# Sums with the unit matrix kept in the order of the text on VectorE, in a two-layer graph network kernel

## The chip, the cores and the metric

The kernel runs on one core of a Trainium2 chip. The metric is the device time of one execution in microseconds (us), and the median of three runs is given. A profile of one more execution shows what each engine did: TensorE (PE, with its weight loads as PEld), VectorE (DVE), ScalarE (ACT), GpSimd (POOL) and SyncE (SP), which issues most DMAs. All data are float32.

## The reference, cut to what matters

The input is x, 128 graphs of 128 nodes with 256 channels, and adj, an adjacency matrix of 128 x 128 for each graph. There are two layers, each with a layer norm and a residual around it. Layer 0 joins a convolution over the nodes, a message-passing product and a gated recurrent unit, for all nodes. Layer 1 touches the first 25 nodes of each graph. It works on five groups of them (25, 9, 7, 6 and 6 nodes), and each group has two graph convolutions with normalised adjacency:

```python
A = adj + jnp.eye(n, dtype=adj.dtype)
deg = jnp.sum(A, axis=-1)
...
norm_adj = dinv[:, :, None] * A * dinv[:, None, :]
support = jnp.einsum('bnd,de->bne', x, W)
out = jnp.einsum('bnm,bme->bne', norm_adj, support) + b
return jax.nn.relu(out)
```

The sum adj + eye is what the change is about. It is needed twice: once for the first convolution and once for the second.

## The kernel before, in words

The 128 graphs are worked on in 32 blocks of four graphs. A first phase (up to about 440 us) makes the convolution of layer 0 by way of spectra; it is not touched here. Then comes a loop over the 32 blocks. For each block `gates(i, ...)` computes the recurrent unit in four units (`unit`, lines 709 to 743): each is a product by Strassen's scheme, seven sums of matmuls (line 719), each in its own PSUM bank. What comes out of a bank goes to ACT (`m1`, line 722, and `m5`, line 730), DVE (lines 724, 727, 734, 737, 740) and POOL (lines 732, 738). There are eight banks, and a matmul that opens a bank has to wait until the former content was read. The first unit of a block writes tile `o` (or `r`), followed by a sigmoid in two halves on ACT (line 755); the next ones write `nh`, `nn` and `z`.

Between the seven sums of a unit, `step()` lets other work go on, all of it written as Python generators: `beside_gates` (the messages, the edge terms, the convolution's output and, in `back`, the end of the block two before) and, once all blocks of a part are done, `layer1` of that part. The parts have 40, 40, 36 and 12 graphs (`PARTS`), so that layer 1 of a part runs beside the gates of a few later blocks, and the last part at the very end. Blocks beside which no layer 1 runs are called plain blocks here.

`back(i, ae, dc)` prepares layer 1 of a block: it adds the residual (line 860), takes the first 25 nodes out (`xl`, line 870), and then adds the unit matrix `ie` to the block's edges `ae` (line 876, 100 x 212) and scales the five groups of it by `dinv` (line 879). A few steps later it makes the layer norm of these nodes (lines 886 to 892: statistics on DVE, a power on POOL, a product on ACT into `hn`), multiplies `hn` by `ae` on PE (line 896) and scales the result (line 901). `ae` has one buffer; it is loaded on SP (line 851) as soon as the L896 of the block before has read it.

In `layer1` the second convolution goes by packs: 60 diagonal blocks of graphs of one group, at most 128 wide. `prepare(j)` (lines 911 to 928) does three things when pack j's turn comes: it issues the load of adjacency `nt` of pack j+8 (line 918) and of its scale `dck` (line 921) on SP, and on DVE it adds the unit matrix `ident` to pack j+2's `nt` (line 925) and multiplies it by `dck` (line 926). `last` reads `nt` in a matmul (line 967), adds bias and relu on ACT (line 970), and sums into `f` on DVE (line 975). Line 987 is the matmul of the first convolution, line 1046 that of the second's support.

The order of the instructions on each engine is not the text's alone. A planner places them when the program is built: an instruction whose inputs it takes as ready may float ahead of others on its engine. `tc.keep_in_program_order(ins)` pins one behind what the text has issued last on the same engine. On POOL the whole first phase and a few more places are in the order of the text. At run time each engine works through its own queue in order.

The wrappers that the change touches, as they stand before:

```python
nc.vector.tensor_add(ae[:n4], ae[:n4], ie[:n4])
...
ops = [nc.vector.tensor_add(nt[:n, :n], nt[:n, :n], ident[:n, :n]),
       nc.vector.tensor_mul(nt[:n, :n], nt[:n, :n], dc[:n, :n])]
tc.keep_in_program_order(ops[1])
```

Here the product (`ops[1]`) is pinned behind the sum, and the sum is not pinned.

Of the kernel before, what the change touches and what calls it, by code (L numbers as in the profile page):

```python
# [77 lines left out]
def gnn_kernel(ctx: ExitStack, tc: tile.TileContext, io, out0: bass.AP, out1: bass.AP):  # L78
    nc = tc.nc
# [13 lines left out]
    def bank():  # L93
        pool, n = banks
        if n is None:
            return pool.tile([P, 512], F32, tag="bank", name="bank")
        banks[1] = (n + 1) % 8
        return pool.tile([P, 512], F32, tag=f"bank{n}", name="bank")
# [10 lines left out]
    ident = cst.tile([P, P], F32)  # L109
# [670 lines left out]
    n4 = BB * NN  # L780
# [5 lines left out]
    ie = l1.tile([P, GW], F32)  # L786
# [69 lines left out]
    def back(i, ae, dc):  # L856

        xt, o = xts.pop(i), outs.pop(i)
        for c in range(C):
            nc.vector.tensor_add(xt[:, c, :], xt[:, c, :], o[:, c, :])  # L860
        xv = xt.rearrange("p c (b n) -> p c b n", b=BB)
        k, b0 = where[i]
        if k == LAST:
            if not kept:
                kept["f"] = l1.tile([P, C, PARTS[k], NN], F32, tag="fl", name="fl", bufs=1)
                kept["ax"] = l1.tile([P, C, PARTS[k] // BB * GW], F32, tag="axl", name="axl", bufs=1)
            xl = kept["f"][:, :, b0:b0 + BB, :]
        else:
            xl = wk.tile([P, C, BB, NN], F32, tag="xl", name="xl", bufs=2)
        nc.vector.tensor_copy(xl, xv[:, :, :, :NN])  # L870
        yield

        nc.sync.dma_start(out0[i], xv[:, :, :, NN:])
        if k != LAST:
            nc.sync.dma_start(xf[k][:, :, b0:b0 + BB, :], xl)
        nc.vector.tensor_add(ae[:n4], ae[:n4], ie[:n4])
        for g in range(len(GROUPS)):
            av = ae[:n4, GOFF[g]:GOFF[g + 1]]
            nc.vector.tensor_scalar(av, av, dinv[:n4, E0 + 5 * i + g:E0 + 5 * i + g + 1], None, op0=ALU.mult)
        yield  # L880
        ps = bank()
        for c in range(C):
            nc.tensor.transpose(ps[:n4, c * P:(c + 1) * P], xl[:, c].rearrange("p b m -> p (b m)"), ident)
        st = l1.tile([P, 6], F32, tag="st", name="st", bufs=2)
        mv = l1.tile([P, 4], F32, tag="mv1", name="mv1", bufs=2)
        nc.vector.bn_stats(st[:n4], ps[:n4, :D])
        nc.vector.bn_aggr(mv[:n4, 0:2], st[:n4])
        nc.vector.tensor_scalar(mv[:n4, 2:3], mv[:n4, 1:2], EPS, None, op0=ALU.add)
        nc.gpsimd.tensor_tensor(mv[:n4, 3:4], mv[:n4, 2:3], mhalf[:n4, 0:1], op=ALU.pow)
        hn = l1.tile([P, D], F32, tag="hn", name="hn", bufs=1)  # L890
        nc.vector.tensor_scalar(hn[:n4], ps[:n4, :D], mv[:n4, 0:1], 0.0, op0=ALU.subtract, op1=ALU.max)
        nc.scalar.mul(hn[:n4], hn[:n4], mv[:n4, 3:4])
        yield
        ps = bank()
        for c in range(C):
            nc.tensor.matmul(ps[:, c * GW:(c + 1) * GW], hn[:n4, c * P:(c + 1) * P], ae[:n4], start=True, stop=True)  # L896
        if k == LAST:
            ab = kept["ax"][:, :, b0 // BB * GW:(b0 // BB + 1) * GW]
        else:
            ab = l1.tile([P, C, GW], F32, tag="ab", name="ab", bufs=1)  # L900
        nc.vector.tensor_tensor(ab, ps[:, :C * GW].rearrange("p (c m) -> p c m", c=C),
                                dc[:, None, :].to_broadcast([P, C, GW]), op=ALU.mult)
        if k != LAST:
            for g, (s, _) in enumerate(GROUPS):
                at = PARTS[k] * GOFF[g] // BB + b0 * s
                nc.sync.dma_start(xa[k][:, :, at:at + BB * s], ab[:, :, GOFF[g]:GOFF[g + 1]])
        yield
# [3 lines left out]
    def prepare(j):  # L911

        a = j + AHEAD
        if 0 <= a < NPK:
            s, nb = GROUPS[PACKS[a][1][0]][0], PACKS[a][1][2]
            n = nb * s
            nt = l1.tile([P, P], F32, tag="nt", name="nt", bufs=AHEAD + 4)
            ins = nc.sync.dma_start(nt[:n, :n], io["adjN"][a, :n, :n])
            tc.keep_in_program_order(ins)
            dc = l1.tile([P, P], F32, tag="dck", name="dck", bufs=AHEAD)  # L920
            nc.sync.dma_start(dc[:n, :n], dvk[a, :n].partition_broadcast(n))
            loads1[a] = n, nt, dc
        if 0 <= j + 2 < NPK:
            n, nt, dc = loads1.pop(j + 2)
            ops = [nc.vector.tensor_add(nt[:n, :n], nt[:n, :n], ident[:n, :n]),
                   nc.vector.tensor_mul(nt[:n, :n], nt[:n, :n], dc[:n, :n])]
            tc.keep_in_program_order(ops[1])
            ready[j + 2] = nt

    def weights(ws, name, bufs, shape, upto):  # L930
# [13 lines left out]
    def layer1(k):  # L944
# [56 lines left out]
        if k == 0:  # L1001
            weights1(3)
            weights2(3)
            for q in (-2, -1):
                prepare(q)
# [9 lines left out]
        for n, chunk in enumerate(chunks):  # L1015
# [12 lines left out]
            for t in range(len(segs) + 1):  # L1028
                if t < len(segs):
                    g, m0, _ = segs[t]  # L1030
                    m1 = bounds[t + 1]
                    if k == LAST:
                        xv = kept["ax"].rearrange("p c (b m) -> p c b m", m=GW)
                        xv = xv[:, :, :, GOFF[g]:GOFF[g + 1]]
                    else:
                        xv = axs[n][:, :, m0:m1]
                    yield from first(g, m0, m1, xv)
                if t:
                    g, _, packs = segs[t - 1]
                    for b0, nb, at, jj in packs:  # L1040
                        prepare(jj)
                        n1 = nb * GROUPS[g][0]
                        nt = ready.pop(jj)
                        ps = bank()
                        for q in range(HID // P):
                            nc.tensor.matmul(ps[:n1, :D], hh[:, q, at:at + n1], w2s[k5 + g][:, q, :],  # L1046
                                             start=q == 0, stop=q == HID // P - 1)
                        s2 = l1.tile([P, D], F32, tag="s2", name="s2", bufs=3)
                        nc.scalar.mul(s2[:n1, :], ps[:n1, :D], dinv[:n1, K0 + jj:K0 + jj + 1])
                        if late:  # L1050
                            late.pop(0)()
                        late.append(partial(last, g, b0, nb, s2, nt))
                        if jj == ends[g]:
                            weights2(k5 + g + 4)
                        yield
# [10 lines left out]
    def beside_gates(i):  # L1066

        ends = back(i - 2, *back_loads(i - 2)) if i > 1 else iter(())
        if i < NBLK:
            parts = messages(i)  # L1070
            next(parts)
            yield
            next(parts)
            next(ends, None)
            yield
            next(ends, None)
            yield
            edge_terms(i)
            next(ends, None)
            yield  # L1080
            for _ in range(3 if i > 1 else 0):
                yield
            next(ends, None)
            yield
            pss = short_rows(i)
            yield
            for _ in conv_out(i, pss):
                yield
            yield from x_nmp(i)
        for _ in ends:  # L1090
            yield
            if i == NBLK:
                yield
# [42 lines left out]
    for i in range(NBLK):  # L1136
# [28 lines left out]
        if (i + 2) * BB == PARTS[0]:  # L1165
            for q in range(-AHEAD, -2):
                prepare(q)
        for k in range(len(PARTS)):
            if i * BB == first_of[k + 1]:
                layer1s.append(layer1(k))  # L1170

    end = back(NBLK - 1, *back_loads(NBLK - 1))
    next(end)
    for steps in (6, 4):
# [145 lines left out]
```

## Time and profile before

| what | value |
|---|---|
| median of three runs (lowest, highest) | 1830.15 us (1829.33, 1830.82) |
| the profiled execution's own time | 1828.48 us |
| its span, first to last instruction | 1826.6 us |
| granted TensorE clock | 0.999 |
| L876 `ae` sum on DVE | 32 times, 366 to 381 ns |
| L879 `ae` scale on DVE | 160 times, 222 to 798 ns, median 234 |
| L925 `nt` sum on DVE | 60 times, 221 to 772 ns, median 278 |
| L926 `nt` product on DVE | 60 times, 218 to 817 ns, median 280 |

Times inside the profile are counted from the first instruction. A line of the groups or the timeline names the source line, the engine, the operation, the tile written and those read (`o<-bank,u`), the shapes and the count. An idle time in square brackets or after a bar is the engine's idle time just before, with what is held to have ended it; where an instruction waits for several things, the view names one of them. Matmuls are pipelined: float32 matmuls show as two passes, a pass of 128 x 256 lasts 379 ns in the records, and the next one starts before it has ended, so starts tell more than the busy share.

### The profile page before, as it was taken

What the parts mean: (1) busy time and instruction counts of PE and PEld (TensorE: products, weight loads), DVE (VectorE), ACT (ScalarE), POOL (GpSimd) and SP (SyncE); (2) the same over time, 40 slices, a digit from 0 to 9 for tenths busy, and PEclk for the clock granted to TensorE, in tenths of its full rate; (3) what the DMA queues carried; (4) which work ended last, traced back from release to release, by engine and by line L of the source; (5) the groups of instructions that cost most, each with busy time, mean ns of one, the idle gap of its engine ahead of it and who ended that gap; (6) DMA issues with size and microseconds to landing.
All of it is one profiled execution on the core that took longest, in us unless ns stands there. A gap on an engine that the chain in (4) does not pass through costs nothing.

```text
span 1826.6 us, 34568 instructions
## 1 busy us (share of the span) xinstructions
PE 1807.0 (99%) x12552; PEld 1565.5 (86%) x12552; DVE 1359.7 (74%) x3248; ACT 737.4 (40%) x1626; POOL 789.0 (43%) x993
## 2 busy tenths in 40 slices
PE   9999999999999999999999999999999999999998
PEld 7888888888888888888788888888788888888787
DVE  6989956787978878877665687878656677887552
ACT  5766721113433433343344434343343433333334
POOL 4777765774354435443221244344313244444100
PEclk9999999999999999999999999999999999999999
DMA  7989889996533343433243433334434434332034
GB/s 292 354 327 340 336 304 322 344 307 211 144 80 74 79 96 74 92 100 94 64 111 104 121 85 85 72 82 110 88 82 91 132 84 94 74 84 73 22 90 139
DMA packets 279869, 267.46 MB, mean 146 GB/s; under 512 B 170870, under 2 KB 247371, under 8 KB 277651
## 3 DMA queue, kind: packets, MB, share of 16 engines
q1 hardware_dynamic: 272211, 211.67, 41.6%
q10 hardware_dynamic: 7488, 53.58, 7.5%
q8 instruction: 100, 1.64, 0.4%
q14 instruction: 70, 0.57, 0.1%
HBM read 168.84 MB, written 96.35 MB: 145 GB/s over the span
## 4 chain that ended last, share of the span: by engine, by line
PE 90%; DVE 4%; DMA 2%; POOL 1%; SPq 1%; issue 1%; ACT 1%; ACTq 0%; DVEq 0%; POOLq 0%
PE bank L719 43%; PE bank L377 6%; PE bank L256 6%; PE bank L1046 6%; PE bank L987 5%; PE bank L620 5%; PE bank L372 3%; PE bank L670 3%; PE bank L599 3%; PE bank L182 2%; PE bank L285 2%; PE bank L967 1%; PE bank L240 1%; PE bank L896 1%; DMA nt<-in_adjN_dram 1%
## 5 line engine op out<-in xcount | busy, mean ns | idle before, releaser
L732 POOL TENSOR_TENSOR u<-u,m 128x256 f32<-128x256 f32 x128 | 95.1, 743 | 458.6 <-ACT m L730 397.0
L719 PE MATMUL bank<-t,sw 128*128 128x256 f32 x1152 | 291.8, 380 | 0.7 <-DVE nn L734 0.3
L719 PEld LDWEIGHTS bank<-t,sw 128*128 128x128 f32 x1152 | 214.5, 190 | 33.6 <-issue 2.8
L719 PE MATMUL bank<-t,wih 128*128 128x256 f32 x768 | 200.2, 383 | 0.0
L719 PEld LDWEIGHTS bank<-t,wih 128*128 128x128 f32 x768 | 143.1, 190 | 29.3 <-DVE o L759 5.3
L369 POOL TENSOR_TENSOR vs<-v 128x256 f32<-128x256 f32 x134 | 101.6, 783 | 53.8 <-PE bank L372 26.0
L256 PE MATMUL bank<-wc,ht 128*128 128x256 f32 x512 | 124.4, 391 | 0.3 <-issue 0.3
L719 PE MATMUL bank<-xc,wih 128*128 128x256 f32 x384 | 114.8, 380 | 0.1
L719 PE MATMUL bank<-t,whh 128*128 128x256 f32 x384 | 114.5, 380 | 0.0
L719 PE MATMUL bank<-xn,wih 128*128 128x256 f32 x384 | 114.2, 379 | 0.0
L1046 PE MATMUL bank<-w,hh 128*125 128x256 f32 (+9 forms) x480 | 113.4, 380 | 0.1
L719 PE MATMUL bank<-ht,whh 128*128 128x256 f32 x384 | 110.4, 380 | 0.1
L603 ACT ACTIVATE xc<-xc,bn 128x512 f32<-128x512 f32 x64 | 46.2, 722 | 158.6 <-DVE xc L602 158.5
L643 ACT ACTIVATE msg<-msg 128x512 f32<-128x512 f32 x64 | 36.8, 622 | 179.3 <-DVE msg L639 179.3
L256 PEld LDWEIGHTS bank<-wc,ht 128*128 128x128 f32 x512 | 93.9, 191 | 16.2 <-issue 0.7
L1046 PEld LDWEIGHTS bank<-w,hh 128*125 128x125 f32 (+9 forms) x480 | 84.4, 178 | 18.2 <-DVE hh L992 1.2
L987 PE MATMUL bank<-ax,w 128*128 128x500 f32 (+9 forms) x352 | 94.5, 404 | 0.9 <-DVE xc L602 0.9
L772 ACT ACT_TABLE_LOAD x31 | 39.8, 1283 | 117.0 <-DVE z L740 117.0
L737 DVE TENSOR_TENSOR u<-bank,u 128x256 f32<-128x256 f32 x128 | 53.4, 417 | 44.9 <-PE bank L719 44.5
L374 ACT COPY k<-bank 128x256 f32<-128x256 f32 x67 | 24.9, 372 | 145.9 <-PE bank L372 76.2
L719 PEld LDWEIGHTS bank<-xn,wih 128*128 128x128 f32 x384 | 72.9, 190 | 10.0
L719 PEld LDWEIGHTS bank<-xc,wih 128*128 128x128 f32 x384 | 72.1, 190 | 9.8 <-ACT m L722 1.9
(225 smaller groups left out, 4563.9 us busy)
## 6 DMA issues: line engine op xcount, KB each, us to landing
vd<-sp ACTq DMA_DIRECT2D x16, 2176.0 KB
v<-vd SPq DMA_DIRECT2D x34, 1024.0 KB
w<-in_w_dram SPq DMA_DIRECT2D x40, 512.0 KB
ln<-in_x_dram SPq DMA_DIRECT2D x32, 512.0 KB
htd<-ht SPq DMA_DIRECT2D x32, 512.0 KB
yd<-ys ACTq DMA_DIRECT2D x32, 512.0 KB
ht<-htd SPq DMA_DIRECT2D x64, 256.0 KB
ym<-yd SPq DMA_DIRECT2D x32, 512.0 KB
```

What stands on the lines that cost most here:

```text
L256: nc.tensor.matmul(pv[:, s, :], ht[:, c, (2 * h + s) * N:(2 * h + s + 1) * N], wc1[:, c, :], start=c == 0, stop=c == C - 1)
L369: nc.gpsimd.tensor_tensor(vs[:, c], vi[c], vr[c], op=ALU.subtract)
L372: nc.tensor.matmul(p1[:, :D], a[:, c], vs[:, c], start=c == 0, stop=c == C - 1)
L377: nc.tensor.matmul(ps[:, k * D:(k + 1) * D], u[:, c], w[c], start=c == 0, stop=c == C - 1)
L599: nc.tensor.matmul(ps[:, b * N:(b + 1) * N], ym[:, 2 * h + b, o * P:(o + 1) * P], idm, start=False, stop=b == 1)
L620: nc.tensor.matmul(ps[:, b, :], d[:, b * N:(b + 1) * N], w, start=True, stop=True)
L670: nc.tensor.matmul(ps[:, b * N:(b + 1) * N], msg[:, b, c * P:(c + 1) * P], e[:, b, :], start=True, stop=True)
L719: nc.tensor.matmul(ps, w, d, start=n == 0, stop=n == len(pairs) - 1)
L732: nc.gpsimd.tensor_tensor(got["u4"], got["u2"], got["m5"], op=ALU.add)
L737: nc.vector.tensor_tensor(got["u3"], ps, got["u2"], op=ALU.add)
L987: nc.tensor.matmul(pv[:, q - q0, :], w1s[k5 + g][:, c, q * P:(q + 1) * P], xv[:, c], start=c == 0, stop=c == C - 1)
L1046: nc.tensor.matmul(ps[:n1, :D], hh[:, q, at:at + n1], w2s[k5 + g][:, q, :], start=q == 0, stop=q == HID // P - 1)
```

## The change

The sum of `ae` and `ie` and that of `nt` and `ident` are both pinned in the order of the text. The product in `prepare` was pinned already and stays so. Nothing is added to or taken from the work. The text of the change has one line less, so lines after 925 are one lower in it (L967 becomes L966); lines are named by the numbers of the kernel before unless said otherwise.

```diff
@@ -873,7 +873,7 @@
         nc.sync.dma_start(out0[i], xv[:, :, :, NN:])
         if k != LAST:
             nc.sync.dma_start(xf[k][:, :, b0:b0 + BB, :], xl)
-        nc.vector.tensor_add(ae[:n4], ae[:n4], ie[:n4])
+        tc.keep_in_program_order(nc.vector.tensor_add(ae[:n4], ae[:n4], ie[:n4]))
         for g in range(len(GROUPS)):
             av = ae[:n4, GOFF[g]:GOFF[g + 1]]
             nc.vector.tensor_scalar(av, av, dinv[:n4, E0 + 5 * i + g:E0 + 5 * i + g + 1], None, op0=ALU.mult)
@@ -922,9 +922,8 @@
             loads1[a] = n, nt, dc
         if 0 <= j + 2 < NPK:
             n, nt, dc = loads1.pop(j + 2)
-            ops = [nc.vector.tensor_add(nt[:n, :n], nt[:n, :n], ident[:n, :n]),
-                   nc.vector.tensor_mul(nt[:n, :n], nt[:n, :n], dc[:n, :n])]
-            tc.keep_in_program_order(ops[1])
+            tc.keep_in_program_order(nc.vector.tensor_add(nt[:n, :n], nt[:n, :n], ident[:n, :n]))
+            tc.keep_in_program_order(nc.vector.tensor_mul(nt[:n, :n], nt[:n, :n], dc[:n, :n]))
             ready[j + 2] = nt
 
     def weights(ws, name, bufs, shape, upto):
```

## The prediction

> **What bounds the kernel now.** I read the page first. TensorE (PE) is busy for the whole span and VectorE (DVE) for three quarters of it:
>
> ```profile
> PE 1807.0 (99%) x12552; PEld 1565.5 (86%) x12552; DVE 1359.7 (74%) x3248; ACT 737.4 (40%) x1626; POOL 789.0 (43%) x993
> ```
>
> A busy PE may still be a waiting one, so I went on to the busy time by stretches, cut at the first L896 matmul of neighbouring blocks (columns: length, then busy time of PE, PEld, DVE, ACT, POOL). 36.12 us is the length of most blocks in which no layer-1 work runs. Three of those shown are longer:
>
> ```profile
> 705.42:741.53 36.11, 36.11 (x211) 32.20 (x210) 29.41 (x67) 14.01 (x28) 15.71 (x20) 1.00 0.35 80
> 741.53:781.08 39.55, 37.64 (x212) 32.03 (x211) 33.32 (x83) 13.89 (x28) 16.69 (x20) 1.00 0.39 88
> ...
> 1248.14:1285.39 37.25, 36.84 (x212) 32.03 (x211) 30.27 (x71) 13.89 (x28) 16.58 (x20) 1.00 0.45 120
> 1644.04:1682.53 38.49, 37.38 (x212) 32.11 (x210) 30.00 (x71) 13.89 (x28) 16.25 (x20) 1.00 0.29 78
> ```
>
> In the plain blocks PE is tight: the chain of the end runs through PE alone there, and its longer pieces hold 18 passes of L719 in 3.89 us or 24 in 5.18 us, 0.216 us each in both. So a DVE delay that reaches PE is lost time, and there is little to win: about 8 us, in the long blocks, as worked out below. What makes them long is in the waits of DVE (total, times, longest):
>
> ```profile
> DVE nt L925 <- DMA nt<-in_adjN_dram: 50.2, 27, 4.5
> ...
> DVE ae L876 <- DMA ae<-in_adjE_dram: 9.4, 7, 2.9
> ```
>
> **What the change moves.** It adds and removes no instruction. Set against each other, the two built programs have the same order on PE, ACT and POOL. On DVE the six instructions of `ae` (L876 and five L879) and the 60 pairs L925/L926 stand elsewhere; on SP the `dck` loads (L921) come later, because each waits for the L926 that frees its buffer.
>
> *The place of ae.* In the plain blocks before, the six stand between L727 and L587 of the next-gate unit (1107.9 us in the block I follow). In the change they stand 28 us later, in the next block, between L734 and L737 of the first gate unit (tile `o`). So I priced the new place with the rows of that place before. First the length of the set, from DVE's timeline, where POOL is idle beside it and where it is not:
>
> ```profile
> 1034.70 0.37 DVE L876 TENSOR_TENSOR ae<-ae,ie 100x212 f32<-100x212 f32 x1
> 1035.11 0.85 DVE L879 TENSOR_SCALAR ae<-ae,dinv 100x100 f32<-100x100 f32 x5
> 1035.87 0.42 DVE L587 TENSOR_TENSOR e<-e,at 128x256 f32<-128x256 f32 x1
> ```
> ```profile
> 1107.92 0.37 DVE L876 TENSOR_TENSOR ae<-ae,ie 100x212 f32<-100x212 f32 x1
> 1108.32 1.37 DVE L879 TENSOR_SCALAR ae<-ae,dinv 100x100 f32<-100x100 f32 x5
> 1109.61 0.41 DVE L587 TENSOR_TENSOR e<-e,at 128x256 f32<-128x256 f32 x1
> ```
>
> Start to next start: 1.17 us alone; 1.69 us when one L879 stands still (752 ns instead of about 230) until POOL's L732 ends at 1109.52. Now the new place, in the timelines of DVE, POOL, ACT and PE:
>
> ```profile
> 1099.75 0.42 DVE L734 TENSOR_TENSOR o<-bank,u 128x256 f32<-128x256 f32 x1 [1.12 <-PE bank L658]
> 1100.10 0.41 DVE L737 TENSOR_TENSOR u<-bank,u 128x256 f32<-128x256 f32 x1
> ```
> ```profile
> 1098.99 0.73 POOL L732 TENSOR_TENSOR u<-u,m 128x256 f32<-128x256 f32 x1 [3.17 <-ACT m L730]
> 1100.59 0.73 POOL L738 TENSOR_TENSOR o<-u,m 128x256 f32<-128x256 f32 x1 [0.87 <-DVE u L737]
> ```
> ```profile
> 1101.35 0.72 ACT L755 ACTIVATE o<-o,brz 128x512 f32<-128x512 f32 x1 [0.16 <-POOL o L738]
> 1101.98 0.35 ACT L722 COPY m<-bank 128x256 f32<-128x256 f32 x1
> 1102.44 0.51 ACT L892 ACTIVATE hn<-hn,mv 100x256 f32<-100x256 f32 x1
> ```
> ```profile
> 1102.80 0.59 PE L719 MATMUL bank<-xc,wih 128*128 128x256 f32 x2
> ```
>
> DVE has 1.12 us of idle time here, but before L734, and the set comes behind it. (The view names PE; by its wait list L734 also needs POOL's L732, which ends at 1099.72.) POOL's next work, L738, needs L737, so POOL is idle while the set runs: I take 1.17 us. Then every step is pushed by 1.17, because each starts close behind what it waits for (0.08 us, 0.03, and ACT's own pace): L737 1101.27, L738 1101.76, the second half of L755 1102.52, and L722 behind it on ACT's queue 1103.15 to 1103.50. L722 needs nothing of `ae`; it is merely queued. But it empties a PSUM bank, and the matmul of 1102.80 waits for that bank by the program's list. Its spare time before is 1102.80 - 1102.33 = 0.46 (unrounded), and 0.05 is what always lies between a release and the matmul (the least I found). PE stops for 1.17 + 0.05 - 0.46 = **0.76 us**. The others in the queue ask less: the bank freed by L737 has 0.99 spare (0.23 lost), that of L740 0.90 (0.32), `hn` (L892, 0.71 spare before L896) 0.51; these run together, the largest counts. Nothing gives it back: later in the block DVE waits for PE again (1.71 us before L737 at 1118.68), so the next block starts alike. The room at the old place is worth nothing, as PE never waited there.
>
> *How often.* L734 has that idle time of 1.1 us in 24 blocks (0 to 10, 14 to 20, 24 to 29). The spare time of L722 is 0.44 to 0.48 in 17: 17 x 0.76 = 12.9. Blocks 0, 19 and 27 have 0.23, 0.34 and 0.09: 0.99 + 0.88 + 1.13 = 3.0. Blocks 8, 20 and 29 had 0.05, but late through L925 waits that go: 3 x 0.76 = 2.3. Block 10 gets two pairs (0.8 us) just ahead of L651, which has 0.70 spare: 0.9. Together **+19.1 us**. In the other eight blocks DVE waits 0.2 to 2.6 us for ACT or PE between L734 and L886 (block 31: 2 us at L992), and the first L896 has 1.7 to 9 us spare: nothing.
>
> *What the pairs give back.* Before, the eight L925 of 751 to 760 us wait for loads just issued (2.80 and 0.66 us) and 16 short instructions run in one block: 39.55 - 36.12 = 3.43. Likewise 1.13 (1248) and 2.37 (1644). Block 10 took 36.79, of which I give back 0.5. PE's longest single stop after that, 0.7 at 1298.0 (for L602), follows the 4.5 us wait. At the start `ae` leaves the `dinv` chain, for which PE waited 0.6 at L835: 0.4. Sum **-8.5**. The `ae` waits (9.4 us in 7 times) go too, but lie in these or in blocks where PE does not wait.
>
> *What the pairs cost in their new place.* By the neighbours' times before, each L926 still stands 6 us or more ahead of the L967 that reads its `nt`, with the loads issued eight packs ahead: no new DMA wait. Parts 0 and 1 keep their pairs in three layer-1 blocks each (16 before, 18 after between 854 and 1031 us), where DVE is idle for 60.59 - 36.94 = 23.7 us, 23.3 and 20.4. I take 0; uncovered, two more pairs of about 0.5 us in each of three parts are 3 us; below nothing there is only the gain counted above. The later `dck` loads on SP stand before `ht`, `xt`, `ae` and `nt` loads; those are wanted tens of us later (`ae` in the change 28 us after its issue, `yr` 68 us in the block followed): 0.
>
> **Sum.** +19.1 - 8.5 = +10.6 us on the profiled execution (1828.48 us, span 1826.6): 1839.1. That execution lies 1.67 below the median of the runs, so I forecast 1830.15 + 10.6 = **1840.7 us**, 0.6% slower.
>
> A rule that speaks against this: the Trainium skill, "Perfetto Trace Analysis", section "Identifying the Most-Contended Engine", says that matmul busy time is a bad measure of distance to the limit, and that weight-load busy time is the better one. In a plain block that is 32.20 of 36.11 us, so by the page some 11% would be free, an estimate of 3.9 us a block, the 0.76 would vanish in it, and only the -8.5 would stay. The trace differs: the passes start 0.216 us apart whoever frees the banks, so that room can't be used, and I go by that row.
>
> **Rivals.**
> 1. *The set is slowed by POOL in its new place too.* Then it costs 1.69 to 1.74 and PE 1.28 to 1.33 a block: 24 x 0.55 = 13 more, 1854. For: it was so in most blocks before. Against: POOL waits for L737. 9%.
> 2. *The delay doesn't reach PE*: faster. The place is L722 on ACT. If the push that arrives there is under 0.41 us, no bank is late and only the gain of the pairs stays: 1830.15 - 8.5 = 1821.7. For: L722 needs no DVE result. Against: it stands behind L755 on ACT, in both programs. 13%.
> 3. *Both halves meet.* PE loses 0.35 a block (the push is half absorbed): 24 x 0.35 = 8.4 against 8.5, 1830. 10%.
> 4. *The gain of the pairs doesn't come*, because they crowd DVE in the layer-1 blocks: +19.1, and up to 3 more, 1849 to 1852. 8%.
>
> That the change does nothing is excluded by the built order. The forecast has 60%, spread over 1835 to 1847.
>
> **Numbers.** A measurement can tell 0.2% (3.7 us) from no change. Slower: 60 + 9 + 8 = 77%; same 10%; faster 13%. The range is 1829 to 1854: it takes in both prices of the set and the pairs without gain, and leaves out rival 2 and some of 3 and 1.
>
> **What would show it.** In the profile after: plain blocks of 36.9 us instead of 36.12, all alike; a PE stop of about 0.76 us at the L719 that follows L722 (or charged to ACT's `m`), a few us before L896; L738 and L755 starting 1.2 us later after L734; blocks 8, 20 and 29 as long as the others; the DMA waits of L925 and L876 gone; L879 at 0.23 us each. Plain blocks of 36.12 would prove step one wrong, of 37.4 would prove rival 1, and long layer-1 blocks rival 4.

## The result and the profile after

The change takes 1842.76 us (median of four runs, 1840.76 to 1844.08), beside 1830.49 (1829.33 to 1831.25) for the kernel before in the same session: a ratio of 1.0069, with a 95% interval of 1.0053 to 1.0085. It is 0.7% slower. The profiled execution has a span of 1839.0 us at a granted clock of 0.998, 12.4 us more than the span before.

The busy times, from the page of the change, tell next to nothing. PE gains 9 us of busy time with the same number of instructions, because matmuls whose bank comes late are shown longer (0.70 us instead of 0.59 for a line of two passes, below); DVE is busy 5 us less than before:

```profile
PE 1816.4 (99%) x12552; PEld 1560.8 (85%) x12552; DVE 1354.5 (74%) x3248; ACT 741.1 (40%) x1626; POOL 788.1 (43%) x993
```

The shares of the chain that ended last, from the same page, tell more. Before, that chain ran through PE for 90% of the span, DVE 4%, POOL and ACT 1% each. Now it leaves PE:

```profile
PE 74%; DVE 16%; POOL 3%; ACT 3%; issue 2%; DMA 2%; DVEq 0%; SPq 0%; ACTq 0%; POOLq 0%
```

The same cut into blocks as in the prediction (first L896 to first L896; length, then busy time of PE, PEld, DVE, ACT, POOL). These are blocks 7, 8, 10, 20 and 29 of the change; blocks 7 and 8 answer to the first two lines shown of before, and blocks 20 and 29 to the last two:

```profile
711.75:748.75 37.00, 36.74 (x211) 31.96 (x210) 29.00 (x67) 14.10 (x28) 15.79 (x20) 1.00 0.33 77
748.75:785.75 37.00, 36.76 (x212) 31.96 (x211) 29.03 (x67) 14.09 (x28) 15.73 (x20) 1.00 0.39 90
822.75:860.36 37.61, 36.80 (x211) 31.88 (x210) 29.78 (x71) 14.09 (x28) 15.93 (x20) 1.00 0.41 109
...
1259.14:1296.13 36.99, 36.74 (x211) 31.96 (x210) 29.03 (x67) 14.09 (x28) 15.73 (x20) 1.00 0.43 113
1657.91:1694.92 37.01, 36.76 (x212) 31.96 (x211) 29.01 (x67) 14.10 (x28) 15.81 (x20) 1.00 0.28 75
```

The long blocks are gone: 8, 20 and 29 are as long as their neighbours, and hold 67 DVE instructions instead of 83 or 71. All neighbours are longer, 37.00 us instead of 36.12. No wait of L925 or L876 for a DMA is left in the list of DVE's waits, which L925 led with 50.2 us; it now begins with waits for PE and ACT.

Now the place itself, in a plain block of the change: the timelines of DVE, POOL, ACT and PE (start, duration, instruction; in square brackets the idle time just before and what is held to have ended it).

```profile
1106.72 0.37 DVE L876 TENSOR_TENSOR ae<-ae,ie 100x212 f32<-100x212 f32 x1
1107.13 0.85 DVE L879 TENSOR_SCALAR ae<-ae,dinv 100x100 f32<-100x100 f32 x5
1107.89 0.42 DVE L737 TENSOR_TENSOR u<-bank,u 128x256 f32<-128x256 f32 x1
```
```profile
1108.39 0.74 POOL L738 TENSOR_TENSOR o<-u,m 128x256 f32<-128x256 f32 x1 [2.04 <-DVE u L737]
```
```profile
1109.16 0.72 ACT L755 ACTIVATE o<-o,brz 128x512 f32<-128x512 f32 x1 [1.34 <-POOL o L738]
1109.79 0.35 ACT L722 COPY m<-bank 128x256 f32<-128x256 f32 x1
```
```profile
1107.69 0.59 PE L719 MATMUL bank<-t,whh 128*128 128x256 f32 x2
1108.37 0.70 PE L719 MATMUL bank<-ht,sw 128*128 128x256 f32 x2
1108.90 0.69 PE L719 MATMUL bank<-t,sw 128*128 128x256 f32 x2
1109.43 0.59 PE L719 MATMUL bank<-t,whh 128*128 128x256 f32 x2
1110.20 0.70 PE L719 MATMUL bank<-xc,wih 128*128 128x256 f32 x2 [0.17 <-ACT m L722]
1110.73 0.59 PE L719 MATMUL bank<-xn,wih 128*128 128x256 f32 x2
```

Read it from the top. The set takes 1.17 us (1106.72 to 1107.89), as at its cheap place before. POOL's idle time before L738 was 0.87 and is 2.04; ACT's before the second half of L755 was 0.16 and is 1.34: both 1.17 or 1.18 more. L722 ends at 1110.14 and the matmul that needs its bank starts 0.06 later.

PE's line must be read by starts. A line holds two passes; at 0.216 us each, the next line should start 0.43 later. It starts 0.68 after 1107.69, a stop of 0.25 at the bank that L737 empties, and 0.77 after 1109.43, a stop of 0.34 at L722's. The lines at 1108.37 and 1108.90 (which opens the bank that L740 empties, 1108.41 to 1108.83) take 0.53 to the next start, not 0.43, and so does that at 1110.20: where a bank came late, the second pass follows the first by 0.31 to 0.32 us. So 0.25 + 0.34 + 3 x 0.10 = 0.89, but for rounding the 0.88 by which the block grew.

The records of the weight loads (PEld) show what goes with the slow second passes:

```profile
1107.48 0.41 PEld L719 LDWEIGHTS bank<-t,whh 128*128 128x128 f32 x2
1108.36 0.30 PEld L719 LDWEIGHTS bank<-ht,sw 128*128 128x128 f32 x2 [0.48 <-DVE u L737]
1108.89 0.30 PEld L719 LDWEIGHTS bank<-t,sw 128*128 128x128 f32 x2 [0.23 <-DVE o L740]
1110.19 0.30 PEld L719 LDWEIGHTS bank<-xc,wih 128*128 128x128 f32 x2 [0.57 <-ACT m L722]
```

In step, a load starts about 0.21 us ahead of its pass (1107.48 for the pass of 1107.69). Where the bank is late, the load waits for it too and starts with the pass or 0.01 before it; the load for the second pass follows 0.11 us later, and that pass another 0.21 after its load. So for one pass the load does not run ahead, which fits the 0.10; no run here varies it by itself. At 1108.90 the pass itself was on its pitch; only its load was late.

The list of PE's waits for the stretch of the 32 blocks shows the place, and hides the price:

```profile
PE bank L719 <- ACT m L722: 4.0, 24, 0.2
```

24 times is the number of blocks that the prediction counted, and L722 is the right name. But 4.0 us is a fifth of the 24 x 0.88 = 21 us that the blocks are longer: ends of matmuls are modelled, so much of a stop is shown as a long matmul. The waits of the weight loads, in the list of the whole profile, hide less. Each of the three banks is late 24 times; before, L722 was named 5 times (1.9 us), L737 twice (0.5 us) and L740 never:

```profile
PEld bank L719 <- ACT m L722: 13.6, 24, 0.6
PEld bank L719 <- DVE u L737: 11.9, 24, 1.1
PEld bank L719 <- DVE o L740: 5.5, 24, 0.2
```

Block lengths in the profiled executions (us):

| block | before | change | e1 | e2 | e3 | e4 | e5 | e6 | e7 | e8 |
|---|---|---|---|---|---|---|---|---|---|---|
| plain | 36.12 | 37.00 | 37.00 | 36.12 | 38.05 | 36.25 | 36.12 | 37.45 | 36.12 | 36.77 |
| 8 | 39.54 | 37.00 | 42.32 | 36.12 | 38.06 | 36.25 | 36.12 | 37.45 | 36.12 | 36.76 |
| 10 | 36.79 | 37.61 | 38.11 | 36.45 | 38.67 | 36.88 | 36.72 | 38.05 | 36.43 | 37.39 |
| 20 | 37.25 | 37.00 | 38.54 | 36.12 | 38.05 | 36.25 | 36.12 | 37.43 | 36.85 | 36.77 |
| 29 | 38.49 | 37.00 | 39.78 | 36.12 | 38.06 | 36.26 | 36.12 | 37.44 | 37.95 | 36.79 |

The first L896 comes at 488.7 us before and at 489.8 to 495.9 in the others, without order: the first phase, which no edit touches, differs by some us from profile to profile. So block lengths are read first here, and medians second.

### The profile page after: what moved, and what is told of

Its sections match the earlier page's. It is cut to its first block, busy times and chain, and to the rows that moved or that the text cites. A ratio compares the mean times of both kernels' runs of the same rounds, so it can differ in the third digit from the quotient of the medians.

```text
span 1839.0 us, 34613 instructions
## 1 busy us (share of the span) xinstructions
PE 1816.4 (99%) x12552; PEld 1560.8 (85%) x12552; DVE 1354.5 (74%) x3248; ACT 741.1 (40%) x1626; POOL 788.1 (43%) x993
## 4 chain that ended last, share of the span: by engine, by line
PE 74%; DVE 16%; POOL 3%; ACT 3%; issue 2%; DMA 2%; DVEq 0%; SPq 0%; ACTq 0%; POOLq 0%
PE bank L719 31%; PE bank L377 6%; PE bank L256 6%; PE bank L1045 6%; PE bank L986 5%; PE bank L599 3%; PE bank L372 3%; PE bank L670 3%; DVE xt L860 2%; PE bank L182 2%; PE bank L620 2%; PE bank L285 2%; DVE o L773 1%; PE bank L966 1%; PE bank L240 1%
## 5 line engine op out<-in xcount | busy, mean ns | idle before, releaser
L732 POOL TENSOR_TENSOR u<-u,m 128x256 f32<-128x256 f32 x128 | 94.8, 740 | 472.5 <-ACT m L730 436.0
L737 DVE TENSOR_TENSOR u<-bank,u 128x256 f32<-128x256 f32 x128 | 53.5, 418 | 69.8 <-PE bank L719 69.7
```

The costliest lines, as they stand in the source:

```text
L732: nc.gpsimd.tensor_tensor(got["u4"], got["u2"], got["m5"], op=ALU.add)
L737: nc.vector.tensor_tensor(got["u3"], ps, got["u2"], op=ALU.add)
```

## The experiments

Three theories were set against each other. Theory A is the prediction's chain: the set pushes L737, L738, L755 and L722 and stops PE by what exceeds the spare time, and the pinned pairs give back the long blocks. Rival B: the stop is not tied to this chain; DVE's work costs in proportion, wherever it stands in this stretch. Rival C: the pinned pairs do nothing, and the long blocks vanish for the sake of `ae`. Each ratio below is to the kernel before in the same session: 1832.16 us for the first four kernels, 1831.44 for the other four.

**The two halves apart.** Only the sum of `ae` pinned, the pairs as before:

```diff
-        nc.vector.tensor_add(ae[:n4], ae[:n4], ie[:n4])
+        tc.keep_in_program_order(nc.vector.tensor_add(ae[:n4], ae[:n4], ie[:n4]))
```

> Only the sum of ae and ie is pinned; the pairs of the packs float as before. Theory A (the cost comes from the set of ae behind L734 in the 24 plain blocks, 0.88 us each by the profile after; the gain comes from the pairs): plain blocks stay at 37.0 us, the long blocks 8, 20 and 29 are long again, and the time is 1842.8 + 8.5 = about 1851 us. Rival C (the long blocks went because ae no longer waits for its DMA, and the pairs do nothing): 1843 us, blocks 8, 20 and 29 at 37.0 us.

Measured: 1855.45 us, ratio 1.0129 (1.0115 to 1.0142). Only the pairs pinned, `ae` as before:

```diff
-            ops = [nc.vector.tensor_add(nt[:n, :n], nt[:n, :n], ident[:n, :n]),
-                   nc.vector.tensor_mul(nt[:n, :n], nt[:n, :n], dc[:n, :n])]
-            tc.keep_in_program_order(ops[1])
+            tc.keep_in_program_order(nc.vector.tensor_add(nt[:n, :n], nt[:n, :n], ident[:n, :n]))
+            tc.keep_in_program_order(nc.vector.tensor_mul(nt[:n, :n], nt[:n, :n], dc[:n, :n]))
```

> Only the pairs are pinned; ae floats as before. Theory A: plain blocks 36.12 us, blocks 8, 20 and 29 as well, time 1830.5 - 8.5 = about 1822 us, faster than both kernels. Rival C (the pairs do nothing): 1830.5 us with the long blocks as before. A third reading (pairs crowd the layer-1 blocks): more than 1830.5 us, with blocks 11 to 13 longer than 60.6, 61.0 and 55.9 us.

Measured: 1822.04 us, ratio 0.9958 (0.9944 to 0.9971): faster than both kernels. The halves have opposite signs, and each does what theory A says of it. With the pairs alone, block 7 and block 8 are alike and plain, with PE busy from end to end:

```profile
706.93:743.05 36.12, 36.12 (x211) 32.20 (x210) 29.42 (x67) 14.02 (x28) 15.74 (x20) 1.00 0.35 75
743.05:779.17 36.12, 36.12 (x211) 32.20 (x210) 29.43 (x67) 14.01 (x28) 15.74 (x20) 1.00 0.39 85
```

With `ae` alone, block 8 is not only long, but longer than before (42.32 instead of 39.54), so rival C falls. These are the DVE timeline there and the head of the whole list of DVE's waits:

```profile
763.05 0.29 DVE L925 TENSOR_TENSOR nt<-nt,ident 125x125 f32<-125x125 f32 x1 [5.97 <-DMA nt<-in_adjN_dram]
```
```profile
DVE nt L925 <- DMA nt<-in_adjN_dram: 67.4, 27, 6.0
```

The longest wait of an L925 in this block was 2.80 us before and is 5.97, and all L925 together wait 67.4 us instead of 50.2. So the halves don't add. By the sums of blocks 1 to 31, `ae` alone makes them 24.7 us longer and the pairs alone 9.1 shorter, together +15.6, and the change has +11.3. (The medians agree, 1.0129 x 0.9958 = 1.0087 beside 1.0069, but that difference is within their intervals.) Why the loads are waited for longer when `ae` moves is not settled.

**The length of the set, shorter and longer.** First without the five L879, next with five more:

```diff
         tc.keep_in_program_order(nc.vector.tensor_add(ae[:n4], ae[:n4], ie[:n4]))
-        for g in range(len(GROUPS)):
-            av = ae[:n4, GOFF[g]:GOFF[g + 1]]
-            nc.vector.tensor_scalar(av, av, dinv[:n4, E0 + 5 * i + g:E0 + 5 * i + g + 1], None, op0=ALU.mult)
```

> The change without the five L879: it leaves out the scaling of the edges by dinv, so that the set behind L734 is L876 alone, 0.41 us from start to start instead of 1.17. Theory A (a push below 0.46 - 0.05 = 0.41 us does not reach PE, since L722 then still empties its bank in time): plain blocks 36.1 to 36.2 us, time 1842.8 - 24 x 0.88 = about 1822 us. Rival B (any DVE work in this stretch costs PE in proportion, 0.88 for 1.17 us): 0.31 us a block, plain blocks 36.4 us, 1829 us.

Measured: 1823.34 us, 0.9956 (0.9942 to 0.9969). The set is now 0.29 us long, under the spare time of 0.41 to the point where PE would stop (DVE timeline):

```profile
1099.94 0.37 DVE L876 TENSOR_TENSOR ae<-ae,ie 100x212 f32<-100x212 f32 x1
1100.23 0.42 DVE L737 TENSOR_TENSOR u<-bank,u 128x256 f32<-128x256 f32 x1
```

Plain blocks are back at 36.12 exactly: an insertion of this length, under the spare time, is free there. In proportion (rival B) it would have been 36.12 + 0.88 x 0.29 / 1.17 = 36.34. Next the longer set:

```diff
             nc.vector.tensor_scalar(av, av, dinv[:n4, E0 + 5 * i + g:E0 + 5 * i + g + 1], None, op0=ALU.mult)
+        for g in range(len(GROUPS)):
+            av = ae[:n4, GOFF[g]:GOFF[g + 1]]
+            nc.vector.tensor_scalar(av, av, 1.0, None, op0=ALU.mult)
```

> The change with five more scalings (by 1.0) behind the five L879, about 0.14 to 0.19 us each from start to start, 0.75 us in all. Theory A (beyond the spare time each us of the set is a us of PE): plain blocks 37.0 + 0.75 = 37.75 us, time 1842.8 + 24 x 0.75 = about 1861 us. Rival B (in proportion): 0.88 x 1.92 / 1.17 = 1.44 instead of 0.88, plain blocks 37.56 us, 1856 us.

Measured: 1853.72 us, 1.0121 (1.0107 to 1.0135). The plain blocks and the time came out below the expectation, and as recorded nearer to rival B's figures than to theory A's, because I priced the added instructions too high: multiplied by a constant, they start 0.09 us apart on average (0.46 us from 1115.73 to 1116.19 for five), against 0.15 for the L879 (0.75 for five), as the DVE timeline shows:

```profile
1114.57 0.37 DVE L876 TENSOR_TENSOR ae<-ae,ie 100x212 f32<-100x212 f32 x1
1114.98 0.85 DVE L879 TENSOR_SCALAR ae<-ae,dinv 100x100 f32<-100x100 f32 x5
1115.73 0.55 DVE L882 TENSOR_SCALAR ae<-ae 100x100 f32<-100x100 f32 x5
1116.19 0.42 DVE L737 TENSOR_TENSOR u<-bank,u 128x256 f32<-128x256 f32 x1
```

The set is 1.62 us, 0.45 more, and the plain block 37.45, also 0.45 more. The added 0.45 us cost PE all of it. In proportion to this set it would be 0.88 x 1.62 / 1.17 = 1.22, or 37.34.

**The innocent instruction in the queue.** Here only ACT's order differs: the L722 of the next unit goes ahead of the second half of the sigmoid. The work of DVE, and the place of `ae` in it, stay as in the change:

```diff
-                    nc.scalar.copy(got["m1"], ps)
+                    copied = nc.scalar.copy(got["m1"], ps)
+                    if second:
+                        tc.keep_in_program_order(copied)
+                        tc.keep_in_program_order(second())
...
+            unit(2, (2,), nh, (1, 2, 6, 5, 3, 7, 4), second=lambda: sigmoid(1))
```

> The change with one swap on ACT: the copy L722 of the next unit goes ahead of the second half of the sigmoid L755, in 30 blocks; the order on all other engines is the same. Theory A (L722 is late only because it is queued behind L755, which waits for POOL and so for the set of ae): the stop at the matmul behind L722 goes, the stops at the banks of L737 and L740 (0.25 + 0.19) stay, and L896 now waits for hn by 0.1 to 0.2; plain blocks 36.7 to 36.8 us, time 1842.8 - 24 x 0.25 = about 1837 us. Rival (the lateness is DVE's alone, ACT's queue plays no part): 37.0 us and 1843 us.

Measured: 1836.82 us, 1.0035 (1.0021 to 1.0049); plain blocks 36.77. The ACT and PE timelines (line 758 is 755 here, 741 is 738):

```profile
1111.47 0.37 ACT L722 COPY m<-bank 128x256 f32<-128x256 f32 x1
1112.90 0.72 ACT L758 ACTIVATE o<-o,brz 128x512 f32<-128x512 f32 x1 [1.06 <-POOL o L741]
```
```profile
1112.11 0.70 PE L719 MATMUL bank<-ht,sw 128*128 128x256 f32 x2
1112.64 0.69 PE L719 MATMUL bank<-t,sw 128*128 128x256 f32 x2
1113.17 0.59 PE L719 MATMUL bank<-t,whh 128*128 128x256 f32 x2
1113.60 0.59 PE L719 MATMUL bank<-xc,wih 128*128 128x256 f32 x2
```

L722 now runs 1.4 us ahead of the second half, and the matmul that waits for it (1113.60) follows the one before by 0.43, without a stop. 0.23 us a block come back, and 0.65 are left. The PE line that starts at 1112.11 is 0.23 late, and it and the one at 1112.64 have slow second passes (0.10 and 0.09). L896 (903 here) starts 0.09 late and has a slow second pass too (0.10). That is 0.61 of it. These are the other members of the queue that the prediction named, the banks of L737 and L740, and `hn`. The list of PEld's waits names them, 24 times each, and no longer L722 (740 here is line 737, 743 is 740, 899 is 892):

```profile
PEld bank L719 <- DVE u L740: 11.8, 24, 1.1
PEld bank L903 <- ACT hn L899: 7.8, 24, 0.3
PEld bank L719 <- DVE o L743: 5.5, 24, 0.2
```

So the wait behind L755 on ACT's queue is shown as a part of the cost. It is not the whole.

**The same six instructions in other places.** In one kernel they stand behind L740, so that they push the statistics of the layer norm instead of L737; in another behind L891, where nothing in a hurry follows. The instructions of the layer norm are pinned in both, so that the places hold:

```diff
+        yield
         tc.keep_in_program_order(nc.vector.tensor_add(ae[:n4], ae[:n4], ie[:n4]))
         for g in range(len(GROUPS)):
             av = ae[:n4, GOFF[g]:GOFF[g + 1]]
-            nc.vector.tensor_scalar(av, av, dinv[:n4, E0 + 5 * i + g:E0 + 5 * i + g + 1], None, op0=ALU.mult)
-        yield
+            tc.keep_in_program_order(nc.vector.tensor_scalar(av, av, dinv[:n4, E0 + 5 * i + g:E0 + 5 * i + g + 1], None, op0=ALU.mult))
...
```

> The change with the set of ae one place later, behind L740 and ahead of L886; all of it pinned. The planner then puts L724 and L727 between the statistics. Theory A (each place has its own price, that of the nearest bank or operand): L722 is on time and PE does not stop there, but hn comes late, by the set and two instructions (1.17 + 0.67 = 1.8 us against 0.71 spare); PE stops once, at L896, by about 1.1 to 1.2 us; plain blocks about 37.3 us, time about 1850 us. Rival B (the set costs the same anywhere in this stretch): 37.0 us and 1843 us.

Measured: 1870.22 us, 1.0220 (1.0206 to 1.0234); plain blocks 38.05. The stop moved to where theory A puts it, ahead of L896 (list of PE's waits, then POOL's timeline):

```profile
PE bank L896 <- ACT hn L892: 40.6, 26, 2.0
```
```profile
1125.94 0.72 POOL L732 TENSOR_TENSOR u<-u,m 128x256 f32<-128x256 f32 x1 [2.33 <-DVE mv L888]
1126.63 0.55 POOL L889 TENSOR_TENSOR mv<-mv,mhalf 100x1 f32<-100x1 f32 x1
```

Its size missed: 1.93 us a block. The set is longer here, 1.41 us from 1123.24 to 1124.65, because L876 (877 here) takes 0.61 us beside POOL's L738 (1122.88 to 1123.62) instead of 0.37, as DVE's timeline shows:

```profile
1123.24 0.61 DVE L877 TENSOR_TENSOR ae<-ae,ie 100x212 f32<-100x212 f32 x1
1123.89 0.85 DVE L880 TENSOR_SCALAR ae<-ae,dinv 100x100 f32<-100x100 f32 x5
1124.65 0.43 DVE L886 BATCH_NORM_STATS2 st<-bank 100x6 f32<-100x256 f32 x1
```

The planner, given the new pins, also put POOL's L732 ahead of the power L889 that `hn` needs. L889's input was there at 1125.86 (end of L888), and it started at 1126.63, 0.77 us later. So this run shows that the stop goes to what hangs behind the set, but it measures three things at once.

```diff
...
         nc.scalar.mul(hn[:n4], hn[:n4], mv[:n4, 3:4])
+        tc.keep_in_program_order(nc.vector.tensor_add(ae[:n4], ae[:n4], ie[:n4]))
+        for g in range(len(GROUPS)):
+            av = ae[:n4, GOFF[g]:GOFF[g + 1]]
+            tc.keep_in_program_order(nc.vector.tensor_scalar(av, av, dinv[:n4, E0 + 5 * i + g:E0 + 5 * i + g + 1], None, op0=ALU.mult))
```

> The change with the set of ae behind L891, around L724 and ahead of L727. Theory A: the sigmoid, L722 and hn are on time; ae itself is ready at about the time of L896 (0.1 late, and 0.1 for the restart); L734 of the second unit waits for POOL in any case and hides the rest. Plain blocks 36.1 to 36.35 us, time 1822 to 1828 us. Rival B: 37.0 us and 1843 us.

Measured: 1825.49 us, 0.9969 (0.9956 to 0.9981); plain blocks 36.25. The set and L724, which slips in, now follow L891 (DVE timeline; in this text 889 is 876, 892 is 879 and 887 is 891):

```profile
1103.65 0.47 DVE L887 TENSOR_SCALAR hn<-bank,mv 100x256 f32<-100x256 f32 x1
1104.04 0.37 DVE L889 TENSOR_TENSOR ae<-ae,ie 100x212 f32<-100x212 f32 x1
1104.32 0.42 DVE L724 TENSOR_TENSOR nh<-bank,m 128x256 f32<-128x256 f32 x1
1104.66 0.84 DVE L892 TENSOR_SCALAR ae<-ae,dinv 100x100 f32<-100x100 f32 x5
```

The same six instructions on the same engine cost 0.88 us a block behind L734, 0.13 two microseconds later, and 1.93 in between (with a longer set, and POOL's L732 in the way as well). That ends rival B.

**Where the give-back comes from.** Of the kernel before, only the sums of the first twelve packs pinned:

```diff
+            first = nc.vector.tensor_add(nt[:n, :n], nt[:n, :n], ident[:n, :n])
+            if j + 2 < 12:
+                tc.keep_in_program_order(first)
```

> The kernel before with the sum pinned for the first 12 of the 60 packs only; ae floats. Theory A (each long block is the burst of pairs in it): block 8 falls from 39.5 to 36.1 us, block 10 to about 36.4, blocks 20 and 29 stay at 37.2 and 38.5 us; time about 1827 us. Rival (the long blocks have one cause in common, so that a part of the pins does nothing or all): 39.5 us as before and 1830.5 us, or all three at 36.1 us and 1822 us.

Measured: 1827.06 us, 0.9977 (0.9968 to 0.9986). Block 8 falls from 39.54 to 36.12, while 20 and 29 stay long (36.85 and 37.95): each long block is a burst of pairs of its own, in which the sums float ahead to loads that have not landed. That 20 and 29 are 0.4 and 0.5 shorter than before, though their packs aren't pinned, is not a matter of order: from 1000 us on, DVE, ACT, POOL, PE and SP have the order of the kernel before. The waits for loads differ. In block 20 DVE waited 1.7 us for the load of `ae` before, and now does not; in block 21 an L925 waits 5.2 us for its load instead of 4.5. Blocks 21 and 23 are 0.6 and 0.7 us longer (61.78 after 61.15, and 56.54 after 55.85). Why those loads land otherwise is open.

## Why the prediction was right, point by point

**The bound.** PE in the plain blocks, tight to its pitch: right. The rule that the prediction weighed against it, by which some 11% would be free there since weight loads are busy for 32.20 of 36.11 us, is not borne out (the page names the share of peak arithmetic beside it, which the prediction left out): above the spare time, 0.45 us more on DVE cost 0.45 us of PE (the longer set).

**The place and the length of the set.** Right: 1.17 us between L734 and L737, with POOL idle beside it and the L879 at 230 to 275 ns (222 to 798 before). Rival 1 falls.

**The push and the spare time.** Right in every step, with 1.17 to 1.18 passed along L737, L738, L755 and L722, and 0.06 to the matmul. The matmul behind L722 is 0.25 + 0.20 + 0.34 = 0.79 us late, where 0.76 was forecast; the smaller stop at L737's bank (0.25, forecast 0.23) is contained in it, as forecast. Rival 2, that the delay doesn't arrive, is refuted by 24 stops named after L722.

**The mis-sized term.** 0.76 a block was 0.88. Behind the stop at L722's bank PE does not take up its pitch at once: the next pass comes 0.10 us later than in step, and this is added. The prediction put that at nothing. The plain blocks of before have no stop, so no row of theirs shows it; the long blocks have seven such slow passes behind a stop (the first of block 8 at 752.07, with 0.32 us to the next), which it did not use.

**How often.** 24 blocks, right. The extra for blocks 0, 19 and 27 did not show in 19 and 27, which became 36.99 and 37.02 like all others; block 0 can't be told from the first phase. Block 10: 0.9 forecast, 37.61 - 36.45 = 1.16 measured against the kernel with only the pairs.

**What the pairs give back.** 3.42, 1.13 and 2.37 us in blocks 8, 20 and 29 in the kernel with only the pairs, as forecast to 0.01; 0.34 in block 10 instead of 0.5. What I undersized are the layer-1 blocks: 0.42 (11), 0.21 (13), 0.97 (21) and 0.20 (23) are 1.8, where I gave 0.7. The 0.4 at the start can't be seen under the first phase's variation.

**What the pairs cost.** No net cost, as taken: the layer-1 blocks are equal or shorter in every one of the eight, so rival 4 falls.

**The sum.** Over blocks 1 to 31: 20.4 up (22 x 0.88 and 1.16), 9.1 down, +11.3; with 1.1 at the start, which may be the first phase's, +12.4 in the span. For the same blocks, without block 0 and the start, the forecast had 18.1 up and 8.1 down, +10.0. Both halves were too small, by 2.3 and 1.0, and partly cancel; that the median is within 2.1 us owes something to this luck. Rival 3, both halves meeting with the push half absorbed, falls: nothing of the push is absorbed beyond the spare time.

## What to carry to other kernels

Pinning an instruction that floats ahead to a load that has not landed pays (here 9 us). The same pin on one that stood well only moves it, and then it cost, in the change and the two kernels with another length of the set, its length less the smallest spare time of all that is queued behind it, on its own engine and on the engines that wait for that, and 0.10 us for the slow pass behind a late bank; nothing where it was shorter than the spare time. So look at what the built order puts directly behind the pinned instruction, and at whether a PSUM bank or an operand of the tight engine hangs on it, even through an instruction that has nothing to do with it. The best version here pins the pairs alone: 1822.04 us.

## What the runs showed of the hardware

Where the bank of a matmul comes late, its first 128 x 256 float32 pass is followed by the second after 0.31 to 0.32 us instead of 0.216, at a granted clock of 1.00 for the stretch. A stop of some tenths thus costs 0.10 more than its length. It was seen at 1108.37, 1108.90 and 1110.20 in the change and at 1112.11 and 1112.64 with the sigmoid's half moved. The records of the weight loads fit it: the load waits for the bank as well and loses its start of about 0.21 us ahead of the pass.

PE's own waits and busy times show little of such stops (4.0 us of 21 in the change); the waits of the weight loads name all three banks, 24 times each.

On DVE, the five small products with a constant start 0.09 us apart on average, and the same five shapes with a scale per partition 0.15 us.

On DVE, the sum of 100 x 212 took 0.61 us beside POOL's 128 x 256 L738, and 0.37 us with POOL idle.
